# A position-bias network on one Trainium2 core: four keys a group, channels sorted by sign, partial sums added by accumulating transfers

## The chip, the core and the metric

The kernel runs on one core of one Trainium2 chip. TensorE (PE), VectorE (DVE), ScalarE (ACT), GpSimd (POOL) and SyncE (SP) run side by side, each in its own instruction order, and wait for one another by semaphores; transfers run on 16 DMA engines that all queues share. All data are 32-bit floats. The metric is the device time of one launch in microseconds (us), lower is better. A profile is one profiled execution.

## What is computed

The program is a chain of four layers on an image batch of 2 x 512 x 32 x 32. The change is in the first layer, a deformable attention with 2 x 8 heads: 1024 query positions look at 64 sampled keys per head. To the scores a bias is added that a small network computes from the distance of each query to each key:

```python
pos = grid_q[:, :, None, :] - grid_kv[:, None, :, :]         # 16 heads x 1024 x 64 x 2
bias = jnp.sign(pos) * jnp.log1p(jnp.abs(pos))
bias = jax.nn.relu(bias @ cpb_w1 + cpb_b1)                   # 2 -> 128
bias = jax.nn.relu(bias @ cpb_w2 + cpb_b2)                   # 128 -> 128
bias = (bias @ cpb_w3 + cpb_b3)                              # 128 -> 1
sim = jnp.einsum('bhid,bhjd->bhij', qh, kh) + bias
attn = jax.nn.softmax(sim, axis=-1)
```

The 128 -> 128 product, for 16 x 64 x 1024 positions, is the large piece of work here.

## The kernel before

Channels lie on the 128 partitions, the 1024 queries along the free axis. `queries_keys_values` (line 618) comes first: it normalizes x, makes the queries `q_pad` (in the large tile `room`), runs a depthwise convolution on DVE and PE, derives the sampling grid, samples by matmuls (`pkv`), makes the keys `kbd` and the values `val`, and writes the signed logarithms of the distances, which separate into an x part and a y part, to DRAM (`feat`). `first_layer` (line 510) loads these parts back, broadcast to all partitions (tiles `ab`, 64 loads of 512 KB from the SP queue), and scales them by the first layer's weights on ACT.

`biased_scores` (line 827) is the position network. Its loop runs over 8 head pairs p, over j = 0, 2, ... 30, and over 4 turns t (two heads, two halves of 32 keys). One turn treats two keys:

- `hidden` (line 864): for each key DVE adds the x and y parts to a tile of 128 x 1024 (L868); ACT rectifies it (L877), or, for 3 in 16, DVE (L875). Six such tiles are kept.
- `second_layer` (line 880): the 128 output channels are taken in two halves of 64. For a half, the two keys' products lie side by side in one PSUM tile `ph`: four matmuls with 128 x 32 weights fill its four blocks of 32 partitions at the same time (L888; such a group of four is called a set below; each 32-bit matmul of the code stands twice in the trace). There are three `ph` tiles of two banks. ACT rectifies the lower half to `lo` (L898) and the upper half to `hi`, scaled by |w3| (L900); DVE adds lo times the rest of w3 (L901).
- `last_layer` (line 904): a product with a 128 x 32 matrix that is zero but for two columns of signs adds a pair's channels into rows j and j+1 of the PSUM tile `sim` (L909). It is done one step of j late, after turn 1.

At j = 16 the product of queries and keys (`scores`, L921) is added into the same PSUM tile; at the end of a head pair DVE stores it with the bias b3 to `simT` (L931). From the fifth head pair on, softmax steps of the finished ones run beside. The order of PE's instructions is as written in the source; for the other engines a scheduler orders them by an estimate of its own, and each engine then takes its list strictly in order. At j = 16 of the last head pair q is used no more, and `load_weights` loads the next stage's weights (out_w, 1 MB, and mlp_w1, 4 MB) into the same large tile.

Of the kernel before, what the change touches and what calls it, by code (L numbers as in the profile page):

```python
# [72 lines left out]
def constants():  # L73
    p = np.arange(128)
    px, py = (p % 32).astype(np.float32), (p // 32).astype(np.float32)
    neg_y = np.stack([-(py + 4.0 * c) for c in range(8)], axis=1).astype(np.float32)
    j = np.arange(64)
    gx, gy = (j % 8).astype(np.float32), (j // 8).astype(np.float32)

    gj = np.stack([gx, gy]).reshape(2, 1, 4, 16).repeat(16, axis=1)  # L80
    gj = gj.transpose(2, 0, 1, 3).reshape(128, 16)
    line = (2.0 * np.arange(32, dtype=np.float32) / np.float32(31) - 1.0).astype(np.float32)
    groups = np.zeros((128, 128), np.float32)
    for g in range(8):
        groups[16 * g : 16 * g + 16, 16 * g : 16 * g + 16] = 1.0 / 16

    y, x = np.divmod(np.arange(HW), 32)
    taps = np.zeros((HW, 9, 2), np.float32)
    for k in range(9):
        taps[:, k, 0] = y + k // 3 - 1  # L90
        taps[:, k, 1] = x + k % 3 - 1
    taps = taps.reshape(8, 128, 18).transpose(1, 0, 2).reshape(128, 144)
    parts = [
        ("ident", np.eye(128, dtype=np.float32)),
        ("groups", groups),
        ("minus", np.broadcast_to(np.array([0.0, -1.0], np.float32), (128, 2))),
        ("neg_xh", -px[:, None] - np.float32(0.5)),
        ("neg_yh", neg_y - np.float32(0.5)),
        ("gx", np.broadcast_to(gx, (128, 64))),
        ("gy", np.broadcast_to(gy, (128, 64))),  # L100
        ("gj", gj),
        ("line", np.broadcast_to(line, (128, 32))),
    ]
    packed, at = _pack(parts)
    return packed, at, taps


def layouts(i):
# [10 lines left out]
    for name in ("cpb_b2", "cpb_w3"):  # L119

        halves = np.asarray(i["L0_conv_" + name]).reshape(2, 64, 1)
        parts.append((name, np.concatenate([_twice(halves[0]), _twice(halves[1])], axis=1)))
# [20 lines left out]
    cst, cst_at, taps = constants()  # L143
# [8 lines left out]
    for h in range(2):  # L152
# [17 lines left out]
        "w2": np.asarray(i["L0_conv_cpb_w2"]),  # L170
# [106 lines left out]
def layers(net, out):  # L277
# [12 lines left out]
    with ExitStack() as later:  # L290
# [12 lines left out]
        with ExitStack() as l0a:  # L303
# [8 lines left out]
            w2 = keys.tile([128, 128], F32, name="w2_t", tag="w2")  # L312
            first = net.pool(l0a, "cpb_ab", 4)
            parts = queries_keys_values(net, bn, simT, q_flat, q_pad, kbd, val, feat, first)
            nc.sync.dma_start(out=w2, in_=net.ins["w2"])

            def load_weights():
                t = new_room()
                w1 = t[:, : 4 * 2048].rearrange("p (k m) -> p k m", m=2048)
                out_w = t[:, 4 * 2048 :].rearrange("p (k m) -> p k m", m=C)  # L320
                nc.sync.dma_start(out=out_w, in_=net.ins["out_w"])
                nc.sync.dma_start(out=w1, in_=net.ins["mlp_w1"])
                return w1, out_w

            w1, out_w = biased_scores(
                net, q_pad, kbd, feat, w2, simT, first, parts, load_weights
            )
# [290 lines left out]
def queries_keys_values(net, bn, simT, q_flat, q_pad, kbd, val, feat, first):  # L618
# [5 lines left out]
    with ExitStack() as ctx:  # L624
# [15 lines left out]
        with ExitStack() as part:  # L640
# [33 lines left out]

            pd = bank("pd")
# [6 lines left out]
            nc.scalar.activation(g, g, AF.Gelu, bias=net.vec("odw_b"))  # L682

        with ExitStack() as part:
# [61 lines left out]

            for gt, name in grids:
                g3 = gt.rearrange("p (n j) -> p n j", j=64)
                base = net.cst(name).unsqueeze(1).to_broadcast([128, NP, 64])
                nc.vector.scalar_tensor_tensor(g3, g3, 4.0, base, ALU.mult, ALU.add)  # L750
# [55 lines left out]
            for w, out, factor in ((kw, kbd, 64**-0.5), (vw, val, 1.0)):  # L806
                for q in range(2):
# [15 lines left out]
                    )  # L823
    return done


def biased_scores(net, q_pad, kbd, feat, w2, simT, first, parts, load_weights):
# [12 lines left out]
    with ExitStack() as ctx:  # L840
        small = net.pool(ctx, "cpb_w", 1)
        hid1 = net.pool(ctx, "cpb_h1", 6)
        lows = net.pool(ctx, "cpb_lo", 2)
        highs = net.pool(ctx, "cpb_hi", 6)
        ps_h = net.psum(ctx, "cpb_ps_h", 3)
        ps_sim = net.psum(ctx, "cpb_ps_sim", 1)
        w3_lo, w3_hi = net.vec("cpb_w3", 0), net.vec("cpb_w3", 1)
        b2_lo, b2_hi = net.vec("cpb_b2", 0), net.vec("cpb_b2", 1)
        sign = small.tile([128, 1], F32, name="sign", tag="sign")
        nc.vector.tensor_scalar(sign, w3_hi, 0.0, 2.0, ALU.is_ge, ALU.mult)  # L850
        nc.vector.tensor_scalar(sign, sign, 1.0, None, ALU.subtract)
        size = small.tile([128, 1], F32, name="size", tag="size")
        nc.vector.tensor_tensor(size, w3_hi, sign, ALU.mult)
        size_b = small.tile([128, 1], F32, name="size_b", tag="size_b")
        nc.vector.tensor_tensor(size_b, size, b2_hi, ALU.mult)
        low_w = small.tile([128, 1], F32, name="low_w", tag="low_w")
        nc.vector.tensor_tensor(low_w, w3_lo, sign, ALU.mult)

        w3 = small.tile([128, 62], F32, name="w3", tag="w3")
        nc.vector.memset(w3, 0.0)  # L860
        nc.vector.tensor_copy(w3[0:64, 30:31], sign[0:64, :])
        nc.vector.tensor_copy(w3[64:128, 31:32], sign[64:128, :])

        def hidden(i, j, on_vector):
            at_x, at_y = parts[i, j % 32 // 16]
            k = 16 * (j // 32) + j % 16
            h1 = hid1.tile([128, HW], F32, name="h1", tag="h1")
            nc.vector.tensor_tensor(  # L868
                h1.rearrange("p (y x) -> p y x", x=32),
                at_x[:, k : k + 1, :].to_broadcast([128, 32, 32]),  # L870
                at_y[:, k, :].unsqueeze(2).to_broadcast([128, 32, 32]),
                ALU.add,
            )
            if on_vector:
                nc.vector.tensor_scalar(h1, h1, 0.0, None, ALU.max)  # L875
            else:
                nc.scalar.activation(h1, h1, AF.Relu)  # L877
            return h1

        def second_layer(pair):  # L880

            phs = []
            for k in range(2):
                ph = ps_h.tile([128, HW], F32, name="ph", tag="ph")
                for n in range(2):
                    for t in range(4):
                        c0 = 64 * k + 32 * (t % 2)
                        nc.tensor.matmul(  # L888
                            ph[32 * t : 32 * t + 32, half(n)],
                            lhsT=w2[:, c0 : c0 + 32],  # L890
                            rhs=pair[t // 2][:, half(n)],
                            start=True,
                            stop=True,
                            skip_group_check=True,
                        )
                phs.append(ph)
            lo = lows.tile([128, HW], F32, name="lo", tag="lo")
            nc.scalar.activation(lo, phs[0], AF.Relu, bias=b2_lo)  # L898
            hi = highs.tile([128, HW], F32, name="hi", tag="hi")
            nc.scalar.activation(hi, phs[1], AF.Relu, bias=size_b, scale=size)  # L900
            nc.vector.scalar_tensor_tensor(hi, lo, low_w, hi, ALU.mult, ALU.add)  # L901
            return hi

        def last_layer(sim, j, sums):


            for n in range(2):
                for t in range(4):
                    nc.tensor.matmul(  # L909
                        sim[32 * t : 32 * t + 32, half(n)],  # L910
                        lhsT=w3[:, 30 - j : 62 - j],
                        rhs=sums[t][:, half(n)],
                        start=(j == 0),
                        stop=(j == 30),
                        skip_group_check=True,
                    )

        def scores(p, sim):
            for n in range(2):
                for t in range(2):  # L920
                    nc.tensor.matmul(  # L921
                        sim[64 * t : 64 * t + 64, half(n)].rearrange("p (y x) -> p y x", x=32),
                        lhsT=kbd[:, p, 64 * t : 64 * t + 64],
                        rhs=q_pad[:, p, 1 + 16 * n : 17 + 16 * n, 1:33],
                        start=False,
                        stop=False,
# [3 lines left out]
        def store(p, sim):  # L930
            nc.vector.tensor_scalar(simT[:, p, :], sim, net.vec("cpb_b3"), None, ALU.add)  # L931
# [16 lines left out]
        hidden_done = 0  # L948
        for p, j in [(p, j) for p in range(NP) for j in range(0, 32, 2)]:
            if j % 16 == 8:  # L950
                nxt = 2 * p + j // 16 + 1
                if nxt < 2 * NP:
                    parts.update(list(first_layer(net, first, feat, *divmod(nxt, 2)))[-1])
            sums = []
            for t in range(4):
                pair = []
                for k in range(2):
                    key = j + 32 * (t % 2) + k
                    pair.append(hidden(2 * p + t // 2, key, hidden_done % 16 in (3, 8, 13)))
                    hidden_done += 1  # L960
                sums.append(second_layer(pair))
# [6 lines left out]
            elif j == 16:  # L968
                scores(p, sim)
                if p == NP - 1:  # L970
                    weights = load_weights()
            pending = (p, j, sums)
            if p >= CC and j % 8 == 4:
                next(beside, None)
        for _ in beside:
            pass
        last_layer(sim, *pending[1:])
        store(NP - 1, sim)
        return weights
# [1184 lines left out]
```

## Time and profile before

| what | before |
|---|---|
| median of 3 runs (range) | 3835.34 us (3830.59 to 3837.44) |
| span of the profiled execution | 3835.8 us |
| mean granted TensorE clock | 0.992 |
| busy, share of the span: PE, DVE, ACT, POOL | 97%, 72%, 67%, 5% |
| position network, first ph matmul to last sim matmul | 86.6 to 2122.2 us |
| DMA: bytes moved, mean rate | 168.57 MB, 44 GB/s |

The span is the time from the first to the last instruction of the profiled execution. In a row of groups stand the source line, the engine, the operation, the tiles (output <- inputs), the shape and the count; behind the bar the busy time in us, the mean time of one in ns, the idle time of the engine just before such instructions, and what ended most of that. In a row of a timeline stand the start in us, the duration in us, the engine, the line and the count. PEld is the load of weights into TensorE, which overlaps matmuls. In the lines of 40 digits each digit is the busy share, in tenths, of one fortieth of the span.

### The profile page before, as it was taken

The page shows a single profiled execution, that of the slowest core. Times are in us where ns is not written, and L with a number is a line of the kernel's source. Part 1 is how long each engine was busy: PE and PEld are TensorE (multiplying, and loading weights), DVE is VectorE, ACT ScalarE, POOL GpSimd, SP SyncE. Part 2 cuts the span into 40 slices and gives each one's busy share as a digit, 9 for nine tenths or more (in the row PEclk, how much of TensorE's full clock was granted, in tenths as well). Part 3 has the DMA queues.
Part 4 walks back from the last instruction along what each step waited for, and adds up shares of the span by engine and source line. Part 5 has one row for each costly group of instructions (what it writes and reads, how often), then busy time and mean ns, then how long its engine had stood idle before and what let it go on. Part 6 is the DMA issues. An engine that isn't in the chain of part 4 may idle for free. (4 is left out here: it accounts for less than half of the span.)

```text
span 3835.8 us, 59384 instructions
## 1 busy us (share of the span) xinstructions
PE 3739.0 (97%) x25356; PEld 1487.3 (39%) x25356; DVE 2765.5 (72%) x3242; ACT 2566.4 (67%) x2941; POOL 189.1 (5%) x180
## 2 busy tenths in 40 slices
PE   7999999999999999999999999999979999899999
PEld 4532222223222322232323444444434544455555
DVE  6999999999999999999999210411475472566565
ACT  7999999999999999999999221211123243345544
POOL 0000000000000000000000000000261150000000
PEclk9999999999999999999999999999999999999999
DMA  3000000000000000000000100112455481000000
GB/s 111 1 23 23 23 1 23 23 23 12 12 23 23 12 12 23 23 12 12 23 23 34 61 0 0 40 61 77 143 185 173 140 276 42 1 12 1 1 20 25
DMA packets 54459, 168.57 MB, mean 44 GB/s; under 512 B 4804, under 2 KB 10436, under 8 KB 51252
## 3 DMA queue, kind: packets, MB, share of 16 engines
q1 hardware_dynamic: 31556, 83.77, 6.2%
q0 software_dynamic: 21776, 79.14, 6.2%
q8 instruction: 200, 3.28, 0.4%
q10 hardware_dynamic: 864, 1.86, 0.2%
q14 instruction: 63, 0.52, 0.0%
HBM read 156.11 MB, written 8.65 MB: 43 GB/s over the span
## 5 line engine op out<-in xcount | busy, mean ns | idle before, releaser
L888 PE MATMUL ph<-h,w_t 128*32 128x512 f32 x16384 | 1808.0, 593 | 15.7 <-ACT lo L898 6.5
L868 DVE TENSOR_TENSOR h<-ab 128x1024 f32<-128x1024 f32 x1024 | 1206.0, 1219 | 67.2 <-PE ph L888 66.2
L888 PEld LDWEIGHTS ph<-h,w_t 128*32 128x32 f32 x16384 | 547.6, 110 | 1239.9 <-issue 1017.2
L877 ACT ACTIVATE h<-h 128x1024 f32<-128x1024 f32 x832 | 872.1, 1067 | 45.6 <-DVE h L868 42.9
L901 DVE SCALAR_TENSOR_TENSOR hi<-lo,low_w,hi 128x1024 f32<-128x1024 f32 x512 | 654.8, 1279 | 31.6 <-ACT hi L900 30.3
L900 ACT ACTIVATE hi<-ph,size_b,size 128x1024 f32<-128x1024 f32 x512 | 621.3, 1214 | 16.7 <-PE ph L888 12.5
L898 ACT ACTIVATE lo<-ph,vec_t 128x1024 f32<-128x1024 f32 x512 | 571.8, 1117 | 5.8 <-PE ph L888 5.4
L2086 ACT ACTIVATE e<-pl,m 128x1024 f32<-128x1024 f32 x128 | 143.6, 1122 | 228.9 <-DVE m L2078 228.9
L1567 PE MATMUL po<-fold,turned 128*128 128x512 f32 x576 | 266.1, 606 | 3.2 <-DVE dfacc L1575 2.9
L2078 DVE TENSOR_REDUCE m<-pl 128x1 f32<-128x1024 f32 x128 | 150.7, 1219 | 147.2 <-PE pl L1988 147.2
L1135 ACT ACTIVATE h<-ph,vec_t 128x512 f32<-128x512 f32 x64 | 44.0, 687 | 312.0 <-PE ph L1127 311.5
L909 PE MATMUL sim<-hi,w 128*32 128x512 f32 x2048 | 251.0, 592 | 0.0
L1127 PE MATMUL ph<-xn,room 128*128 128x512 f32 x512 | 230.9, 594 | 0.0
L1116 PE MATMUL acc<-h,mlp_w_t 128*128 128x512 f32 x512 | 229.8, 592 | 0.0
L1514 DVE SCALAR_TENSOR_TENSOR sum<-got,wts,sum 128x256 f32<-128x256 f32 x432 | 184.4, 478 | 48.8 <-ACT sum L1510 46.4
L1490 POOL DMA_INDIRECT got<-table,idx x144 | 175.0, 1215 | 554.9 <-DVE sum L1514 268.0
L2040 PE MATMUL pt<-cst_t,e 128*128 128x128 f32 x1024 | 149.3, 279 | 6.6 <-ACT aT L2051 4.0
L2040 PEld LDWEIGHTS pt<-cst_t,e 128*128 128x128 f32 x1024 | 118.6, 142 | 93.6 <-issue 61.3
L1567 PEld LDWEIGHTS po<-fold,turned 128*128 128x128 f32 x576 | 106.6, 195 | 112.4 <-issue 107.4
L1116 PEld LDWEIGHTS acc<-h,mlp_w_t 128*128 128x128 f32 x512 | 97.3, 190 | 122.5 <-issue 122.0
L1127 PEld LDWEIGHTS ph<-xn,room 128*128 128x128 f32 x512 | 96.6, 191 | 117.7 <-issue 117.1
L1541 ACT COPY turned<-pt 128x512 f32<-128x512 f32 x72 | 41.9, 582 | 143.8 <-PE pt L1535 143.6
(250 smaller groups left out, 2711.6 us busy)
## 6 DMA issues: line engine op xcount, KB each, us to landing
ab<-feat_d SPq DMA_DIRECT2D x64, 512.0 KB, 4.0
room<-in_dc_w_dram SPq DMA_DIRECT2D x9, 1024.0 KB, 4.8
dc_w_t<-in_dc_w_dram SPq DMA_DIRECT2D x5, 1024.0 KB, 5.3
room<-in_mlp_w_dram SPq DMA_DIRECT2D x1, 4096.0 KB, 15.6
mlp_w_t<-in_mlp_w_dram SPq DMA_DIRECT2D x1, 4096.0 KB, 12.5
dc_w_t<-in_dc_w_dram SPq DMA_DIRECT2D x8, 512.0 KB, 5.0
w_qkv_t<-in_w_qkv_dram SPq DMA_DIRECT2D x3, 1024.0 KB, 8.6
out_dram<-x_all SPq DMA_DIRECT2D x12, 256.0 KB, 2.0
```

What stands on the lines that cost most here:

```text
L868: nc.vector.tensor_tensor(h1.rearrange("p (y x) -> p y x", x=32), at_x[:, k : k + 1, :].to_broadcast([128, 32, 32]), at_y[:, k, :].unsquee ...
L877: nc.scalar.activation(h1, h1, AF.Relu)
L888: nc.tensor.matmul(ph[32 * t : 32 * t + 32, half(n)], lhsT=w2[:, c0 : c0 + 32], rhs=pair[t // 2][:, half(n)], start=True, stop=True, skip_ ...
L898: nc.scalar.activation(lo, phs[0], AF.Relu, bias=b2_lo)
L900: nc.scalar.activation(hi, phs[1], AF.Relu, bias=size_b, scale=size)
L901: nc.vector.scalar_tensor_tensor(hi, lo, low_w, hi, ALU.mult, ALU.add)
L909: nc.tensor.matmul(sim[32 * t : 32 * t + 32, half(n)], lhsT=w3[:, 30 - j : 62 - j], rhs=sums[t][:, half(n)], start=(j == 0), stop=(j == 30 ...
L1116: nc.tensor.matmul(accs[oc], lhsT=self.w2[:, m, 128 * oc : 128 * oc + 128], rhs=hs[m], start=(m == 0), stop=(m == 15),)
L1127: nc.tensor.matmul(ph, lhsT=self.w1[:, k, 128 * m : 128 * m + 128], rhs=xn[:, k, :], start=(k == 0), stop=(k == CC - 1),)
L1514: nc.vector.scalar_tensor_tensor(t[:, q, :], g[:, s, :], w, t[:, q, :], ALU.mult, ALU.add)
L1567: nc.tensor.matmul(self.out, lhsT=turned[:, at : at + 128], rhs=self.folded.w[k][:, i, :], start=(k == 0 and i == 0), stop=(k == 8 and i = ...
L2040: nc.tensor.transpose(pt[:, 128 * c : 128 * c + 128], e[:, 128 * k : 128 * k + 128], ident)
```

## The change

The network's loop is regrouped, and the second layer's sums are formed in another way.

- **Channels by sign.** A new class `Order` computes on the chip, from w3, a place for each of the 128 channels, so that each quarter of 32 channels can be treated with one rule: quarters 1 to 3 hold, in each of the 32 lanes, channels of one sign of w3, and quarter 0 what is left. |w3| is multiplied into the second layer's weights, which are permuted by a matmul with a 0/1 matrix; the biases and signs are permuted in the same way. This takes some 60 DVE operations on one column, seven small matmuls and two small loads, put among the steps of `queries_keys_values`.
- **Four keys a turn.** j runs in steps of 4. `hidden` makes two keys at once (128 x 2048, six such tiles: three groups deep, five of them in the large tile where q was). `second_layer` makes four PSUM tiles, one for each quarter of channels, with the four keys side by side.
- **Sums.** DVE takes quarter 0 (max with minus the bias, times the sign relation: `lo`), ACT rectifies quarters 1 (`hi`) and 2 (`more`), DVE adds max(quarter 3, minus bias) to `more`. Two transfers issued by GpSimd, which add to their destination, form hi += lo and hi += more; the second is written one group later in the source. What the max form leaves out is a constant, computed once and added at the store.
- **Last layer.** One product for four keys: the 128 x 32 matrix has four columns of signs.
- **Scores.** The products of queries and keys run before the loop, at the end of `queries_keys_values`, are copied to `simT`, and the store adds to them. The large tile is then free for the first layer's tiles.
- **Weights.** out_w is loaded in the last step of the loop, mlp_w1 behind the loop in four parts.

The core of the diff:

```diff
+            for p in range(NP):
+                for n in range(2):
+                    pq = bank("pqk")
+                    for t in range(2):
+                        nc.tensor.matmul(
+                            pq[64 * t : 64 * t + 64, :].rearrange("p (y x) -> p y x", x=32),
+                            lhsT=kbd[:, p, 64 * t : 64 * t + 64],
+                            rhs=q_pad[:, p, 1 + 16 * n : 17 + 16 * n, 1:33],
...
+                    (nc.vector.tensor_copy, nc.scalar.copy)[n](simT[:, p, half(n)], pq)
...
+        def hidden(i, j, at):
+
+            at_x, at_y = parts[i, j % 32 // 16]
+            k = 16 * (j // 32) + j % 16
+            h1 = place(at).rearrange("p (k i) -> p k i", k=2)
+            nc.vector.tensor_tensor(
+                h1.rearrange("p k (y x) -> p k y x", x=32),
+                at_x[:, k : k + 2, :].unsqueeze(2).to_broadcast([128, 2, 32, 32]),
+                at_y[:, k : k + 2, :].unsqueeze(3).to_broadcast([128, 2, 32, 32]),
+                ALU.add,
+            )
+            nc.scalar.activation(h1, h1, AF.Relu)
+            return [h1[:, k, :] for k in range(2)]
+
+        def quarter(quad, q):
+            ph = ps_h.tile([128, HW], F32, name="ph", tag="ph")
+            for n in range(2):
+                for t in range(4):
+                    nc.tensor.matmul(
+                        ph[32 * t : 32 * t + 32, half(n)],
+                        lhsT=order.w2[:, 32 * q : 32 * q + 32],
+                        rhs=quad[t][:, half(n)],
...
+        def rectified(ph, q, pool, name):
+            t = pool.tile([128, HW], F32, name=name, tag=name)
+            nc.scalar.activation(t, ph, AF.Relu, bias=order.bias[:, q : q + 1])
+            return t
+
+        def second_layer(quad, late):
+
+            t0 = lows.tile([128, HW], F32, name="lo", tag="lo")
+            nc.vector.tensor_scalar(
+                t0, quarter(quad, 0), order.first, order.low, ALU.max, ALU.mult
+            )
+            total = rectified(quarter(quad, 1), 1, highs, "hi")
+            nc.gpsimd.dma_start(out=total, in_=t0, accum_op=ALU.add)
+            flush(late)
+            more = rectified(quarter(quad, 2), 2, adds, "more")
+            nc.vector.scalar_tensor_tensor(
+                more, quarter(quad, 3), order.floor, more, ALU.max, ALU.add
+            )
+            late.append((total, more))
+            return total
+
+        def flush(late):
+            for total, more in late:
+                nc.gpsimd.dma_start(out=total, in_=more, accum_op=ALU.add)
+            late.clear()
...
         def store(p, sim):
-            nc.vector.tensor_scalar(simT[:, p, :], sim, net.vec("cpb_b3"), None, ALU.add)
+            nc.vector.scalar_tensor_tensor(
+                simT[:, p, :], sim, order.const, simT[:, p, :], ALU.add, ALU.add
+            )
...
-        for p, j in [(p, j) for p in range(NP) for j in range(0, 32, 2)]:
+        late = []
+        slots = list(range(6))
+        for p, j in [(p, j) for p in range(NP) for j in range(0, 32, 4)]:
...
+            if (p, j) == (NP - 1, 28):
+                slots.remove(4)
+                load_out()
             sums = []
             for t in range(4):
-                pair = []
-                for k in range(2):
+                quad = []
+                for k in range(0, 4, 2):
                     key = j + 32 * (t % 2) + k
-                    pair.append(hidden(2 * p + t // 2, key, hidden_done % 16 in (3, 8, 13)))
-                    hidden_done += 1
-                sums.append(second_layer(pair))
+                    quad += hidden(2 * p + t // 2, key, slots[0])
+                    slots.append(slots.pop(0))
+                sums.append(second_layer(quad, late))
                 if t == 1 and pending is not None:
                     last_layer(sim, *pending[1:])
...
+            biased_scores(net, feat, order, simT, first, parts, t, load_out)
+            for k in range(4):
+                nc.sync.dma_start(out=w1[:, k, :], in_=net.ins["mlp_w1"][:, k, :])
```

The buffers: two `lo` tiles, three `more` tiles, seven `hi` tiles, three `ph` tiles as before.

## Prediction

> **What bounds the kernel now.** I read the page first: its slices say which stretch the change is in and which engines are full there.
>
> ```profile
> PE   7999999999999999999999999999979999899999
> DVE  6999999999999999999999210411475472566565
> ACT  7999999999999999999999221211123243345544
> DMA  3000000000000000000000100112455481000000
> ```
>
> A slice is 95.9 us. From the second to the 22nd all three compute engines are at nine tenths and the DMA engines idle: this is the position network, over half the span. Next its groups, in the page's list (count, total busy, mean ns, idle before):
>
> ```profile
> L888 PE MATMUL ph<-h,w_t 128*32 128x512 f32 x16384 | 1808.0, 593 | 15.7 <-ACT lo L898 6.5
> L868 DVE TENSOR_TENSOR h<-ab 128x1024 f32<-128x1024 f32 x1024 | 1206.0, 1219 | 67.2 <-PE ph L888 66.2
> L877 ACT ACTIVATE h<-h 128x1024 f32<-128x1024 f32 x832 | 872.1, 1067 | 45.6 <-DVE h L868 42.9
> L901 DVE SCALAR_TENSOR_TENSOR hi<-lo,low_w,hi 128x1024 f32<-128x1024 f32 x512 | 654.8, 1279 | 31.6 <-ACT hi L900 30.3
> L900 ACT ACTIVATE hi<-ph,size_b,size 128x1024 f32<-128x1024 f32 x512 | 621.3, 1214 | 16.7 <-PE ph L888 12.5
> L898 ACT ACTIVATE lo<-ph,vec_t 128x1024 f32<-128x1024 f32 x512 | 571.8, 1117 | 5.8 <-PE ph L888 5.4
> L909 PE MATMUL sim<-hi,w 128*32 128x512 f32 x2048 | 251.0, 592 | 0.0
> ```
>
> TensorE waits 15.7 us in front of 16384 matmuls: it sets the stage's time, with the other two just behind. The 593 ns is a latency of overlapping matmuls; the rate is in the timeline (start, duration, count) and the slack in the stretch of stages (PE, PEld, DVE, ACT busy):
>
> ```profile
> 2101.38 7.07 PE L888 MATMUL ph<-h,w_t 128*32 128x512 f32 x64
> 2108.27 1.90 PE L909 MATMUL sim<-hi,w 128*32 128x512 f32 x16
> 2109.99 7.05 PE L888 MATMUL ph<-h,w_t 128*32 128x512 f32 x64
> ...
> 500.00:1000.00 500.00, 496.95 (x4590) 147.41 (x4584) 475.25 (x431) 487.26 (x477) 0.00 (x0) 1.00 0.06 18
> ```
>
> From 2101.38 to 2108.27 64 matmuls pass: 6.89/16 = 0.43 us for a set of four side by side. The stage runs from 86.6 (first ph) to 2122.2 (last sim). A pair of keys costs (32+4)/4 = 9 sets, 3.87 us; 512 pairs 1981 us. The 64 L921 matmuls (8 in 1.72 us) add 13.8, the softmax transposes of four head pairs 9.4. That is 2004 of 2035.6 us: 31 us are stalls.
>
> **The change, part by part.** All sums are against this execution, span 3835.8 us, which the median of the runs (3835.34) equals.
>
> Matmuls. The second layer keeps its 16384. The last layer takes four keys instead of two: 2048 become 1024. Four keys then take (64+4)/4 = 17 sets, 7.31 us, where two pairs took 7.74: 256 x 0.43 = 110 us off the engine that sets the end. The L921 matmuls leave the loop: 13.8 more.
>
> DVE, for four keys. Two additions over 2048: 512 elements take 0.69 us (L782) and 1024 take 1.219, so 2048 about 2.28. The first quarter from PSUM as L931 (1024 from PSUM, 1.28). The fourth quarter, PSUM plus SBUF: L1075 takes 0.75 where an SBUF operation of 512 takes 0.69, so 1.28 to 1.34. In all 7.12 to 7.18 us, against 7.31 of PE. Hidden, by 0.13 us only; where it slips, the ph banks hold PE back, as L898 does now.
>
> ACT. Two rectifications over 2048: 0.61 us at 512, 1.067 at 1024, so 1.97; two quarters at 1.117; 0.27 for the ab tiles (64 x 1.22 over 256). 6.45 of 7.31: hidden, with 0.9 us to spare, where before it had none. The stalls of 31 us I keep: DVE is now as near to PE as ACT was.
>
> Stage start. About 60 operations on one column, some 0.1 us apart where the old ones stand (83.9 to 85.7), stand among the DVE's convolution and grid steps, which are on the path: +5 us (bounds 2 and 9). The 64 score matmuls with their copies now run before the loop: +13.8. The first-layer tiles lie where q was, so the first addition waits for the last score matmul, and the first group needs two tiles: 2 x 2.28 + 1.97 = 6.5 us, where 3.4 passed from the last pk matmul (83.3) to the first ph (86.6). Start 86.6 + 5 + 13.8 + 3.2 = 108.6, so +22.
>
> Stage end. The last group's sum must come back from two transfers: about +3 us. SP's loads: out_w is queued 29 us before its use and took 4.8; w1's four parts and then mlp_w_t move behind the loop. 8 MB took 15.6 + 12.5 us before; their readers start 34 and 41 us after the stage's end (2156.0 and 2162.9). Cost 0; without that cover some 15 us.
>
> The transfers. 512 accumulating transfers of 512 KB, issued by GpSimd: nothing like them runs before. In the built program GpSimd's order is strict: lo of a group, more of the same group, lo of the next. The source puts more one group later; the scheduler has moved it forward. "more" waits for the landing of its group's "lo", and behind it on GpSimd stands the next group's "lo". So the least cycle is: more is issued, its bytes move, the next lo's bytes follow on the same engines, land, and free the next more. It has these rows:
>
> ```profile
> got<-table,idx POOLq DMA_INDIRECT x144, 5.3
> out_dram<-x_all SPq DMA_DIRECT2D x12, 256.0 KB, 2.0
> out_dram<-x_all SPq DMA_DIRECT2D x8, 128.0 KB, 1.7
> ...
> 2008.00:2026.00 18.00, 18.00 (x173) 5.43 (x169) 15.19 (x15) 15.30 (x15) 0.00 (x0) 1.00 0.72 292
> 2700.00:3000.00 300.00, 264.89 (x863) 126.61 (x862) 166.36 (x357) 69.85 (x127) 95.40 (x70) 0.95 0.50 166
> ```
>
> A GpSimd issue took 0.94 us with 0.3 between two (the gathers). 128 KB to 256 KB adds 0.3 us to 1.7, so 1.4 is fixed. Cycle = 0.94 + 0.3 + 1.4 + 2X = 2X + 2.6, X being the time of one transfer on all 16 engines. The last two columns are DMA share and GB/s: plain loads moved 292/0.72 = 405 GB/s while busy, gathers of 4 KB rows 166/0.50 = 332. So a plain copy has X = 1.3 to 1.6. An accumulate must read its destination too. The Trainium skill speaks against the change here: "Collectives: The Full Stack", in the section on the bandwidth ceiling, holds that a reduce takes two reads for one write and gets half the rate of a copy; it measured 32.35 GB/s over two engines. By the rows alone, reading hidden: X = 1.6, cycle 5.8, PE's 7.31 stands. By its figure, an estimate: 16.2 GB/s on 16 engines, X = 2.0, cycle 6.6, PE stands. By its rule on this case's rows: X = 2.6 to 3.2, cycle 7.8 to 9.0, and the transfers set the pace. Which it is no row shows. I take X about 2.3 (between the page's own rate and the lower doubling): cycle 7.2, just under PE. Their latency costs nothing below that: lo and hi of a group are done some 6 us after its start, both transfers land by about 18, and the last layer reads them at 3 x 7.31 = 21.9. The 64 ab loads take 0.4 us a group of the same engines (the 5 to 6% share now).
>
> Sum: start +22, loop -110, scores out of the loop -13.8, end +3: -99 us, 3737.
>
> **Rivals.**
> 1. The transfers become the bound. From X = 2.4 the cycle exceeds 7.31; every 0.1 us more costs 256 x 0.2 = 51 us; from X = 2.55 (7.7) the gain of 99 is gone. With the gather row doubled, X = 3.2: cycle 9.0, 256 x 1.69 = 433 more, 4170. At the middle, X = 2.9: 8.4, 4016. For it: GpSimd's blocking order and the skill's rule. Against: a mean share includes the latency of packets, so true X may be lower. That ends slower.
> 2. Accumulation is slower than two reads explain (X of 5 or more, or a descriptor issue of several us): cycle over 12, beyond 4900. No row speaks for it, none excludes it.
> 3. DVE takes PE's place: its 7.18 with a few stalls is 7.4 to 7.5, some 25 to 50 us less gain: 3762 to 3787.
> 4. The stalls vanish, ACT being relieved: 31 us more gain, 3706.
> 5. The start gives it back: that would take 99 us where I find 22 (bounds 19 to 26); not likely.
>
> **How the numbers follow.** PE stays the bound, or nearly (the forecast with rivals 3 and 4; 3706 to 3800): 0.52. Transfers bind gently, ending within 0.2%: 0.03. Rival 1 slower: 0.37. Rival 2: 0.08. 0.2% (8 us) is about what a measurement can tell from no change. Faster 0.52, same 0.03, slower 0.45. The time is that of the likeliest, 3737; its own range is 3706 to 3800. The range runs from 3706 to 4170, the gather row doubled; above lie rival 2 and the worst of rival 1, below little.
>
> **What would show it.** A group's 64 ph matmuls still 0.43 us a set and PE at 99% in the stage: forecast right. PE idle before sim, released by a DMA of hi<-more, or ph waiting for DVE lo that waits for a DMA; GpSimd's issues spaced over 7.3 us: rival 1; the time from issue to landing of hi<-lo decides (under 5.5 us fits, over 7 does not). First ph near 108.6, DVE h near 2.28 us, DVE near 97%. Wrong would be a first ph after 120, a PE gap at the first w1 matmul, or a DVE lagging through other waits than these.

## The result and the profile after

The changed kernel takes 3957.74 us (median of 4 runs, 3950.05 to 3966.92) where the kernel before took 3832.97 us beside it (3829.34 to 3837.44): 1.0327 times as long, 95% interval 1.0309 to 1.0344. The forecast was 3737 us, 99 us less than before. It came out 125 us slower instead, inside the range given, and as the first rival had it.

The slices of the page, as before (a slice is now 98.8 us):

```profile
PE   7999999999999999999999899999988999899999
DVE  7988888888888888888888311410366474566565
ACT  6777777777777777777777221121112233245544
POOL 0122222212122222222222100000143141000000
DMA  3677777776777677767766600012344572000000
```

In the network's stage (second to 23rd slice) DVE fell from nine to eight tenths and ACT from nine to seven, and the DMA engines rose from nothing to seven. PE's digit hides what matters, since 9 stands for all from 90% up. The stretch from 500 to 1000 us tells more (PE, PEld, DVE, ACT, POOL busy, then clock, DMA share, GB/s), with the queue that moves the adding transfers (packets, MB, share of 16 engines):

```profile
500.00:1000.00 500.00, 470.69 (x4120) 143.41 (x4120) 423.50 (x245) 371.11 (x257) 105.81 (x122) 0.99 0.72 143
```

```profile
q0 software_dynamic: 95504, 347.61, 42.3%
```

PE's busy time fell from 496.95 to 470.69 and the matmuls issued in the same time from 4590 to 4120: now all three compute engines wait. The stage runs from the first ph matmul at 104.4 us to the last sim matmul at 2242.9, or 2138.5/256 = 8.35 us for a group of four keys. The forecast had 7.31 for PE and 7.2 for the transfers.

The groups of the stage (busy, mean ns of one, idle before, and what ended most of that):

```profile
L1041 PE MATMUL ph<-room,w_t 128*32 128x512 f32 x13664 | 1860.3, 596 | 80.2 <-DVE lo L1059 34.0
L1028 DVE TENSOR_TENSOR room<-ab 128x2048 f32<-128x2048 f32 x427 | 971.8, 2286 | 190.1 <-PE ph L1041 189.8
...
L1074 POOL DMA_DIRECT2D hi<-more x256 | 219.5, 857 | 1671.7 <-issue 620.4
L1059 DVE TENSOR_SCALAR lo<-ph,floor,low 128x1024 f32<-128x1024 f32 x256 | 342.7, 1339 | 97.5 <-DMA hi<-lo 68.3
...
L1063 POOL DMA_DIRECT2D hi<-lo x256 | 306.4, 1197 | 74.1 <-ACT hi L1053 68.7
...
L1082 PE MATMUL sim<-hi,w 128*32 128x512 f32 x1024 | 188.7, 608 | 65.3 <-DMA hi<-more 65.2
```

The columns behind the second bar tell it. DVE's lo (L1059) waits 68 us for a transfer: there are two lo tiles, and the one it wants is still being read. PE's sim (L1082) waits 65 us for hi<-more. And GpSimd stands 1671.7 us in front of "more" and only 74.1 in front of "lo": its queue moves on only when a "more" may go. Its timeline shows the cycle (start, duration; in brackets the wait before):

```profile
1013.81 0.86 POOL L1074 DMA_DIRECT2D hi<-more  x1 [7.02 <-DVE room L1028]
1014.35 1.21 POOL L1063 DMA_DIRECT2D hi<-lo  x1
1022.66 0.86 POOL L1074 DMA_DIRECT2D hi<-more  x1 [7.11 <-DMA hi<-lo]
1023.20 1.21 POOL L1063 DMA_DIRECT2D hi<-lo  x1
1030.82 0.86 POOL L1074 DMA_DIRECT2D hi<-more  x1 [6.41 <-DVE room L1028]
1031.36 1.21 POOL L1063 DMA_DIRECT2D hi<-lo  x1
```

"more" of a group and "lo" of the next go out together, back to back; then GpSimd stands some 7 us until that lo has landed, and only then the next "more" may go. From one lo to the next it is 8.85 and 8.16 us here. Where the bracket names a DVE addition, the wait is one for several semaphores, and the releaser named is only the event that was last in the record. The sum that a "more" carries was not what was missing: over all 256 groups it had been ready for 8.8 us (median, 1.0 at least) when its "more" was issued, and the data of a "lo" for 6.5 us. After the issues at 1013.81 and 1014.35 the DMA engines are full from 1015.24 to 1020.44, have a share of 0.08 up to 1021.76 and of 0.00 from 1021.80 to 1024.05. So in over 3 of these 8.85 us next to no bytes move, unless loads from the other queue fill the gap, as they did from 1012.95 to 1015.20 (share 0.94).

### The profile page after: what moved, and what is told of

The parts are those of the page before. It is cut to its first block, busy times and chain, and to the rows that moved or that the text cites. A ratio compares the mean times of both kernels' runs of the same rounds, so it can differ in the third digit from the quotient of the medians.

```text
span 3953.9 us, 57067 instructions
## 1 busy us (share of the span) xinstructions
PE 3730.4 (94%) x24348; PEld 1472.7 (37%) x24348; DVE 2647.7 (67%) x2599; ACT 2184.7 (55%) x2118; POOL 635.1 (16%) x692
## 3 DMA queue, kind: packets, MB, share of 16 engines
q0 software_dynamic: 95504, 347.61, 42.3%
## 5 line engine op out<-in xcount | busy, mean ns | idle before, releaser
L1041 PE MATMUL ph<-room,w_t 128*32 128x512 f32 x13664 | 1860.3, 596 | 80.2 <-DVE lo L1059 34.0
L1028 DVE TENSOR_TENSOR room<-ab 128x2048 f32<-128x2048 f32 x427 | 971.8, 2286 | 190.1 <-PE ph L1041 189.8
L1041 PEld LDWEIGHTS ph<-room,w_t 128*32 128x32 f32 x13664 | 530.1, 110 | 1219.2 <-issue 846.6
L1034 ACT ACTIVATE room<-room 128x2048 f32<-128x2048 f32 x427 | 815.5, 1910 | 251.5 <-DVE room L1028 251.3
L1041 PE MATMUL ph<-h,w_t 128*32 128x512 f32 x2720 | 634.2, 594 | 0.2 <-DVE lo L1059 0.2
L1074 POOL DMA_DIRECT2D hi<-more x256 | 219.5, 857 | 1671.7 <-issue 620.4
L1059 DVE TENSOR_SCALAR lo<-ph,floor,low 128x1024 f32<-128x1024 f32 x256 | 342.7, 1339 | 97.5 <-DMA hi<-lo 68.3
L1066 DVE SCALAR_TENSOR_TENSOR more<-ph,floor,more 128x1024 f32<-128x1024 f32 x256 | 327.3, 1278 | 28.6 <-ACT more L1053 22.6
L1063 POOL DMA_DIRECT2D hi<-lo x256 | 306.4, 1197 | 74.1 <-ACT hi L1053 68.7
L1053 ACT ACTIVATE more<-ph,bias 128x1024 f32<-128x1024 f32 x256 | 284.4, 1111 | 51.3 <-PE ph L1041 51.3
L1082 PE MATMUL sim<-hi,w 128*32 128x512 f32 x1024 | 188.7, 608 | 65.3 <-DMA hi<-more 65.2
L1041 PEld LDWEIGHTS ph<-h,w_t 128*32 128x32 f32 x2720 | 175.5, 110 | 111.7 <-issue 109.4
L1028 DVE TENSOR_TENSOR h<-ab 128x2048 f32<-128x2048 f32 x85 | 193.9, 2281 | 0.0
```

Source lines behind the costliest of these rows:

```text
L1028: nc.vector.tensor_tensor(h1.rearrange("p k (y x) -> p k y x", x=32), at_x[:, k : k + 2, :].unsqueeze(2).to_broadcast([128, 2, 32, 32]), a ...
L1041: nc.tensor.matmul(ph[32 * t : 32 * t + 32, half(n)], lhsT=order.w2[:, 32 * q : 32 * q + 32], rhs=quad[t][:, half(n)], start=True, stop=Tr ...
L1053: nc.scalar.activation(t, ph, AF.Relu, bias=order.bias[:, q : q + 1])
L1059: nc.vector.tensor_scalar(t0, quarter(quad, 0), order.first, order.low, ALU.max, ALU.mult)
L1063: nc.gpsimd.dma_start(out=total, in_=t0, accum_op=ALU.add)
L1066: nc.vector.scalar_tensor_tensor(more, quarter(quad, 3), order.floor, more, ALU.max, ALU.add)
```

## The experiments

The theory (A in the expectations) was that the two chained transfers on GpSimd's strict queue set the pace, as in rival 1. Other causes to be told apart were VectorE's in-order work (rival 3), a slow accumulate (rival 2) and SBUF or DMA contention. How much one transfer takes of all 16 engines, X, is read from the queue's share: the gathers of the later stage alone make 6.3% of 3769.1 us = 237 us, so X = (42.3% of 3953.9 us - 237)/512 = 2.80 us in the changed kernel. In its lists of additions, lo and sums DVE has the same order, operation for operation, in the changed kernel and in the next four; ACT's list too is the same in all five.

**Both transfers left out.**

```diff
-            nc.gpsimd.dma_start(out=total, in_=t0, accum_op=ALU.add)
...
-            for total, more in late:
-                nc.gpsimd.dma_start(out=total, in_=more, accum_op=ALU.add)
```

> Leaves both transfers of a group out, so quarters 0, 2 and 3 of the channels are computed but never added to the bias. Theory A (the chain of transfers, 8.3 us a group, sets the loop's time and nothing else in the change does): TensorE is the bound again at 7.31 us a group, 3720 to 3760 us. Rival B (VectorE, relieved of less than I summed, would bind at about the same pace): still 3850 or more, with VectorE over 97% busy in the loop. Rival C (the longer start and end ate the gain): still over 3800 with TensorE at 99% in the loop.

Measured 3771.02 us (3769.79 to 3771.95), ratio to before 0.9842 [0.9825, 0.9858]. So the transfers cost 3957.7 - 3771.0 = 187 us, and the change without them is faster than before. But 34 us above the forecast remain, without any transfer.

**Plain copies, and half the bytes.** Two kernels: the first without `accum_op`, the second with `[:, :512]` on both sides of both transfers.

> The two transfers copy instead of adding (hi is overwritten, the sum is lost); bytes written, instructions, order and waits stay. Theory A (an adding transfer occupies the engines about twice as long as a copy because it reads its destination as well): a transfer falls from about 2.8 us of all engines to about 1.5, the cycle from 8.3 to about 5.6, TensorE binds, 3720 to 3770 us. Rival D (the cycle is fixed latency of issue and landing on GpSimd): within 1% of 3958.

> The two transfers add only the first 512 of 1024 columns (the other half of the sums is left out). Theory A (time of a transfer goes with its bytes): 1.4 us each, cycle about 5.4 us, TensorE binds, 3720 to 3770 us. Rival D (fixed latency): within 1% of 3958. Rival E (cost by packets, not bytes: 128 rows either way): also near 3958, with a DMA share that stays at 0.7.

Measured 3786.46 us, ratio 0.9884 [0.9867, 0.99], and 3787.67 us, ratio 0.9889 [0.9873, 0.9906]: both above the upper end expected, for the reason that still stood open after the kernel without transfers, and 171 us below the changed kernel. The two queue lines, copies first:

```profile
q0 software_dynamic: 95504, 347.61, 23.8%
```

```profile
q0 software_dynamic: 95504, 213.39, 27.1%
```

Bytes and packets of the copies are those of the changed kernel, and the share is 23.8 instead of 42.3%: X = (23.8% of 3784.7 - 237)/512 = 1.30 us for a copy. By this measure adding takes about 2.2 times as long. Half the bytes take (27.1% of 3783.9 - 237)/512 = 1.54 us, 0.55 of 2.80: the cost goes with the bytes, and there is no large fixed price of an adding transfer, so rival 2 falls. A share could count packets that wait, so the packet records are a second measure: from first to last packet, a transfer that runs alone takes 1.44 us as a copy and 1.53 when it adds half the bytes (medians; 2.77 for a whole adding one, in the kernel below with one transfer a group). By the formula of the prediction the cycles are 5.2 and 5.7 us; both are below PE's pace, and both kernels ran at the same time.

**The same transfers in another order.** The whole computation; "lo" of the next group is put ahead of the older "more".

```diff
-            nc.gpsimd.dma_start(out=total, in_=t0, accum_op=ALU.add)
-            flush(late)
+            added = nc.gpsimd.dma_start(out=total, in_=t0, accum_op=ALU.add)
+            with net.tc.issue_after(added.ins):
+                flush(late)
```

> The whole computation. GpSimd is made to issue the next group's lo transfer before the more transfer of the group before, as the source has it, so that more no longer stands waiting in front of it. Theory A1 (the blocking order on GpSimd sets the cycle of 2X + 2.6; the engines alone need only 2X + 0.4 = 6.0 us a group): TensorE or VectorE bind, 3740 to 3800 us, DMA share of the loop near 0.8. Rival A2 (the engines themselves are full, their share of 0.72 hides idle that cannot be used): 3900 or more, GpSimd still waiting for landings over 5 us a group.

Measured 3811.13 us (3806.83 to 3812.95), ratio 0.9943 [0.9926, 0.9959]: bytes, packets and X (2.78) are unchanged, and 147 us are gone. Its stretch and its GpSimd timeline:

```profile
500.00:1000.00 500.00, 485.92 (x4404) 140.81 (x4404) 451.89 (x262) 398.77 (x276) 113.33 (x130) 1.00 0.77 154
```

```profile
1004.46 0.85 POOL L1063 DMA_DIRECT2D hi<-lo  x1 [5.47 <-ACT hi L1053]
1004.99 1.21 POOL L1075 DMA_DIRECT2D hi<-more  x1
1011.67 0.85 POOL L1063 DMA_DIRECT2D hi<-lo  x1 [5.47 <-ACT hi L1053]
1012.21 1.21 POOL L1075 DMA_DIRECT2D hi<-more  x1
```

GpSimd now waits for data (ACT's hi), no longer for a landing: a "lo" goes out 0.3 us after its data are there (median), where it was 6.5. The group's "lo" has had a whole group's time to land when its "more" comes up. So it was not the bytes, 2 x 2.8 = 5.6 us of 7.55, that exceeded PE's time, but the bytes plus the time in which the queue stood: landing, waking, issue, start. It missed the expected 3740 to 3800 by 11 us. The waits show a further price (total, times, longest):

```profile
PEld ph L1041 <- ACT more L1053: 47.0, 32, 2.9
ACT ab L535 <- DMA ab<-feat_d: 44.1, 21, 5.1
```

The ab loads share the 16 engines. Their median from issue to landing is 4.0 us before, 6.1 in the changed kernel, 8.1 here. The scheduler had placed their scaling on ACT right behind the load, a whole block of 16 groups ahead of its use; ACT, in order, stood up to 5.1 us for it, and PE behind ACT. The changed kernel has this wait as well: 43.4 us in all, where it is 1.2 without the transfers.

**The scaling put late.** On top of that order, each of the four scalings of a block goes into one of the last four groups before its use.

```diff
-                    parts.update(list(first_layer(net, first, feat, *divmod(nxt, 2)))[-1])
+                    coming = next(first_layer(net, first, feat, *divmod(nxt, 2)))
...
+                if j % 16 == 12 and nxt < 2 * NP:
...
+                    with net.tc.issue_after(relus[-1]):
+                        nc.scalar.activation(
+                            tile, tile, AF.Identity, bias=bias, scale=net.vec("cpb_w1", a)
+                        )
```

> The whole computation. On top of the reordered transfers (3811, where ScalarE stood 44 us in front of the scaling of ab tiles whose loads landed after 8.1 us instead of 4.0), each scaling is put into the last four groups of a block of 16, a whole block behind its load, one a group. If those waits are what is left of the transfers' cost above the 3771 without them: ACT's wait for DMA ab falls to near 0, PE's wait for ACT more (68 us) to under 20, and the time to 3772 to 3795. If the full DMA engines (share 0.77) hold the loop back in another way, for instance by SBUF traffic slowing the compute engines, the time stays at 3800 to 3815.

Measured 3789.71 us (3787.32 to 3791.99), ratio 0.988 [0.9863, 0.9896], as expected, and the best version of the whole computation: 46 us faster than before, 168 faster than the changed kernel. ACT's wait for the loads is gone, though they land no sooner (8.2 us). Only 19 us are left to the kernel without transfers, at a DMA share of 0.79: by itself this traffic costs the compute engines no more than that.

**One transfer a group.** `more` is added by a DVE operation instead of the second transfer.

```diff
-            flush(late)
...
-            late.append((total, more))
+            nc.vector.tensor_tensor(total, total, more, ALU.add)
             return total
```

> The whole computation with one transfer a group: lo comes by the transfer, the sum of the third and fourth quarter is added by VectorE. The DMA cycle is then 2.8 + 1.9 = about 4.7 us, far under PE's 7.31, and the DMA share falls from 0.72 to about 0.4. If only the transfers held the loop back and VectorE were free, the time would be about 3740 to 3770. But VectorE takes one operation of 1024 elements more, 1.22 us a group: 7.1 + 1.2 = 8.3 us, above PE, so by my account of the engines 256 x 0.7 us over the 3771 without transfers: 3950 to 3990, about the same as with two transfers, with VectorE busy at 0.98.

Measured 3972.45 us (3970.5 to 3975.53), ratio 1.0361 [1.0343, 1.0378], as expected. X is 2.78 again ((23.9% of 3968.7 - 237)/256) and the DMA share 0.37, but DVE is the bound: 481.51 of 500 us busy, and 49 us of the whole kernel it stands for the landing of the one transfer before it can add. So the second transfer is worth having, as long as it doesn't block the first: with both, the best order took 3790.

**What the 34 us without transfers are.** The last layer comes once in four groups. From one sim to the next the kernels without transfers, with the new GpSimd order and with the late scaling show the same time, their most frequent one: 30.2 us for four groups, where their 68 sets take 68 x 0.43 = 29.2. First I took half of lo's work from DVE, with the transfers left out:

```diff
-                t0, quarter(quad, 0), order.first, order.low, ALU.max, ALU.mult
+                t0[:, half(0)], quarter(quad, 0)[:, half(0)], order.first, order.low, ALU.max, ALU.mult
```

> Leaves out both transfers and half the columns of the first quarter's eviction. Without the transfers the loop took 7.6 us a group where 17 sets of matmuls take 7.31, 34 us above the forecast of 3737. Theory: VectorE, with about 7.1 us of work a group in a strict order, evicts late, and PE waits for it (250 us of PEld waits for DVE more and lo, in pieces of 1.5 us). Then 0.6 us a group less of VectorE work brings the loop to about 7.35 us a group, the time to 3715 to 3745, and PE's wait for DVE lo falls by more than half. Rival: PE's loop takes longer for a reason of its own, as gaps in its weight loads or issue; then the time stays at 3762 to 3772.

Measured 3760.98 us, ratio 0.9812 [0.9795, 0.9828]: only 10 us better, and the 30.2 still there (sim at 1023.92, the next at 1054.16), so the amount of DVE's work as such is not what holds PE. But its timeline shows the place:

```profile
1002.49 2.29 DVE L1028 TENSOR_TENSOR room<-ab 128x2048 f32<-128x2048 f32 x1 [2.18 <-PE ph L1041]
...
1004.70 1.28 DVE L1065 SCALAR_TENSOR_TENSOR more<-ph,floor,more 128x1024 f32<-128x1024 f32 x1
...
1006.03 0.11 PEld L1041 LDWEIGHTS ph<-room,w_t 128*32 128x32 f32 x2 [1.05 <-DVE more L1065]
```

DVE has been idle for 2.18 us when PE finishes a group. What it does then is an addition for a later group, which wanted the tile that the group set free; the sum of this group's fourth quarter, ready at the same moment, is queued behind it. Addition 2.29 and sum 1.28 end after 3.5 us, and PE, which has two other ph tiles (2 x 8 sets = 3.44 us), stands about 0.32 us: its sets start 0.75 us apart here (1005.28 and 1006.03) instead of 0.43. The 1.05 in the bracket is the gap between weight loads. Three such stalls in four groups make 30.2 out of 29.2.

**The sum queued ahead of that addition,** with and without the transfers (`mores` holds the sums, one a group):

```diff
-            nc.vector.tensor_tensor(
+            with net.tc.issue_after(mores[-3]) if len(mores) > 2 else ExitStack():
+                nc.vector.tensor_tensor(
```

> The whole computation. In the reordered kernels the loop runs at exactly 30.2 us for four groups (7.55 a group) whether the transfers are there or not, where 68 sets of matmuls take 29.2: three times in four groups TensorE stands 0.32 us in front of a bank that VectorE's sum of the fourth quarter (more) frees late. VectorE has that sum queued behind an addition of a later group, 2.28 us long, which waits for the same last matmuls to free its tile. Here, on top of the reordered transfers and loads (3790), an addition stands behind the sum of the group whose tile it takes. If the order is the cause: four groups in 29.2 to 29.5 us, PE's wait for DVE more under 40 us (178 before), and the time to 3727 to 3750. If VectorE's amount of work is the cause, or the DMA traffic: 3780 to 3795.

> Leaves both transfers out, and has the same order on VectorE: the addition stands behind the sum of the group whose tile it takes. Without the transfers and in the old order it took 3771. If the order on VectorE makes the 34 us between that and the forecast of 3737, it is 3710 to 3740 here; if not, 3765 to 3775. Its distance to the whole computation in the same order is what the transfers cost beside a full PE: 10 to 25 us by the theory that only their place in the queues matters, near 0 or negative by none.

Measured 3810.46 us, ratio 0.9934 [0.992, 0.9947], and 3803.74 us, ratio 0.9918 [0.9903, 0.9933]: both miss the range for the theory by 60 us and more, lie above that for its rival too, and are 21 and 33 us worse than in the old order. The edit did not do what it was meant to: the addition it holds back goes behind the sum, but in 203 and 214 of 256 groups another addition now stands directly before the sum, where it was 254. In DVE's list the order changed to addition, lo, addition, sum, and the waits of the kernel without transfers show a new one:

```profile
DVE more L1068 <- ACT more L1056: 169.7, 127, 2.9
PEld ph L1044 <- ACT hi L1056: 145.2, 179, 2.7
PEld ph L1044 <- DVE lo L1062: 119.8, 108, 2.1
```

DVE now stands in order for ACT, and PE for hi and lo. ACT in turn stands 47.4 us for the ab loads in this kernel, though no transfer slows them: where the scheduler puts the scaling is enough for that. The attempt neither proves nor refutes the chain, since it shortened the stalls (29.9 for four groups, where it went best) and put larger ones elsewhere.

**The same order in the changed kernel.** The edit just shown, and nothing else:

> The whole computation, the changed kernel with nothing but the new order on VectorE; both transfers stand in GpSimd's queue as in the changed kernel, each of more waiting for its lo and the next lo behind it. If that cycle of two transfers, 8.35 us a group, sets the pace, VectorE's order is worth nothing here: 3945 to 3965 where the changed kernel took 3958. If VectorE held it back, 3890 to 3920.

Measured 3939.5 us, ratio 1.0271 [1.0256, 1.0287]: 18 us better than the changed kernel, 5 us below the range expected and far from the 3890 to 3920 that DVE's holding it back would give. The DMA share is again 0.72, and GpSimd's waits in front of "more" are again most of its time. The order on DVE is a small term there.

**The same work taken away at the other place.** Transfers left out, and of one addition in two only 24 of 32 rows. DVE has 0.51 us less to do in a group (249 of 512 additions take 1758 instead of 2281 ns), nearly as much as with the halved lo, 0.53 (804 instead of 1339 ns). The shortened addition is the one directly before the sum, in 240 of 256 groups.

```diff
-                h1.rearrange("p k (y x) -> p k y x", x=32),
+                h1.rearrange("p k (y x) -> p k y x", x=32)[:, :, :rows, :],
```

> Leaves out both transfers and a quarter of one first-layer addition in two (24 rows of 32): VectorE does 0.54 us a group less, as much as in the kernel with the halved lo (3761), but at the place that TensorE waits for: this addition takes the tile that the last matmuls of a group set free, and the sum of the same group's fourth quarter is queued behind it. If that chain (last matmul, addition of 2.28 us, sum of 1.28, bank free 0.32 us late) holds TensorE, shortening it by 0.53 removes the stall: four groups fall from 30.2 to 29.2 to 29.5 us, the time to 3725 to 3745. If the floor of 30.2 has another cause, or is the mere amount of VectorE work, it stays at 3758 to 3768 as with the halved lo.

Measured 3700.76 us (3699.17 to 3706.09), ratio 0.9656 [0.9641, 0.9671]: 70 us less than without the transfers alone, 60 less than with the halved lo. Stretch, two sim rows, and PE's wait for the sum, with the halved lo and here:

```profile
500.00:1000.00 500.00, 500.00 (x4664) 150.58 (x4660) 441.11 (x277) 420.47 (x290) 0.00 (x0) 1.00 0.06 18
```

```profile
1027.16 1.90 PE L1083 MATMUL sim<-hi,w 128*32 128x512 f32 x16
...
1056.34 1.90 PE L1083 MATMUL sim<-hi,w 128*32 128x512 f32 x16
```

```profile
PEld ph L1041 <- DVE more L1065: 177.6, 171, 1.6
PEld ph L1045 <- DVE more L1069: 91.6, 173, 1.1
```

29.18 us for four groups, PE busy 500.00 of 500, and each wait for the sum shorter by about 0.5 us, which the halved lo did not change (179.7 without transfers alone). DVE's order differs from that of the kernel without transfers in 16 of 1024 places, with the halved lo in as many. The same saving on DVE is worth 10 us off the chain and 70 on it. So PE's stalls come from the chain last matmul, addition, sum, ph tile, not from the amount of DVE's work. What was not shown is a whole computation in which a new order alone removes them.

**Seven tiles instead of six,** in the best version:

```diff
-        adds = net.pool(ctx, "cpb_add", 3)
-        highs = net.pool(ctx, "cpb_hi", 7)
-        sixth = net.pool(ctx, "cpb_h1")
+        adds = net.pool(ctx, "cpb_add", 2)
+        highs = net.pool(ctx, "cpb_hi", 6)
+        sixth = net.pool(ctx, "cpb_h1", 2)
...
-        slots = list(range(6))
+        slots = list(range(7))
```

> The whole computation: the reordered transfers and loads (3790) with seven first-layer tiles of 2048 instead of six (one buffer less each for more and for the sums, to make room). An addition then takes a tile that was free some 3.7 us earlier, so it need not start at the end of a group's matmuls, and the sum queued behind it is not late. If that dependence sets the floor of 30.2 us for four groups, it falls to 29.2 to 29.6 and the time to 3735 to 3765; if only the strict order on VectorE matters, which stays the same, or if the scarcer buffers bring waits of their own, 3780 to 3810.

Measured 3801.07 us (3798.95 to 3807.36), ratio 0.9917 [0.9903, 0.993], 11 us worse. DVE's order stayed addition, sum, and the addition again waits for PE's last matmuls; apparently the scheduler used the seventh tile to run one addition further ahead. The time for four groups stayed 30.2, and ACT's more waited 125 us for the scarcer buffers (DMA hi<-more). A version of the whole computation at 29.2 was not found.

## Why the prediction was wrong

The step that failed is "I take X about 2.3 ... cycle 7.2, just under PE": the term X, the time of one adding transfer, was taken too small. It measured 2.80, and with it the transfers, not PE, set the pace of the loop. The form of the sum held: with 2.80 its 2X + 2.6 gives 8.2 us, and the loop took 8.35 a group. The whole sum then gives 3737 + 256 x (8.2 - 7.31) = 3965, where 3958 was measured. Point by point:

- **The cycle's form.** GpSimd's strict order, "more" behind the landing of its "lo", the next "lo" behind that: right. Undoing only this order took away 147 of the 187 us that the transfers cost.
- **The size of X.** Three candidates were set side by side: the rows alone 1.6; 2.0, an estimate from the figure of the Trainium skill ("Collectives: The Full Stack", section "The bandwidth ceiling"); and its rule (a reduce reads twice for one write, so gets half the rate) on this case's rows, 2.6 to 3.2. The measurement is 2.80 against 1.30 for the copy (2.77 and 1.44 from first to last packet): the ratio of about two held, the figure carried over did not (512 KB/16/2.80 us = 11.7 GB/s per engine, where it gave 16.2). That it is the second read that costs, no run here shows. I took a value between the figure and the lower doubling, which no candidate gave. The cycle crosses PE's time at X = 2.4; the doubling of this case's own rows lay wholly above. That was rival 1, given 0.37, and it is what came.
- **"A mean share includes the latency of packets, so true X may be lower".** This argument against rival 1 held for the copy, whose 1.30 lies at the lower end of 1.3 to 1.6, but it could not carry the forecast: this lower end doubled is 2.6, still above 2.4.
- **Matmuls: "17 sets, 7.31 us".** Right as a bound, reached only with the shortened addition (29.18 us for four groups). PE's work fell as said; in the whole computation its waits outweighed that, or in the best order ate about half of the forecast gain (46 us are left of 99).
- **DVE 7.12 to 7.18, "hidden, by 0.13 us only; where it slips, the ph banks hold PE back".** The work was 2 x 2.286 + 1.339 + 1.278 = 7.19, and it slipped. Without transfers the kept 31 us of stalls became 75 (stage 103.6 to 2058.6 us, less 1871 for matmuls and 9.4 for transposes), 44 more; with the addition shortened they are 5 (106.8 to 1992.5). Rival 3 named 25 to 50 us for this and had the wait right; the reason is the place of one operation in the order, not the amount of work.
- **ACT 6.45.** The busy rows give about 6.3; it had the time to spare. (The 0.27 for the ab tiles was a slip: 64 x 1.22/256 is 0.31.) That it would stand in order for the ab loads, slowed by the transfers, I had not seen: their 0.4 us a group was counted as a load on the engines, not as a later landing with ACT behind it. Taking it away was worth 21 us in the kernel with the new order.
- **Start and end.** First ph at 104.4, not 108.6 (+18 instead of +22). From the start of the last sim matmul to the end it is 1711.0 us after and 1714.2 before: the moved weight loads cost nothing, as said.
- **The named check.** For issue to landing of hi<-lo the page gives no figure. The packet records give 6.5 us from issue to last byte (median), and the page of the kernel with only DVE's order changed, where GpSimd has the same order, gives 6.8. That lies between the 5.5 that would fit and the 7 that would not, so this sign alone did not decide. The others did: PE idle before sim, released by hi<-more, and ph waiting for a lo that waits for a transfer.

The gap of 221 us between 3957.7 and 3737 is thus: 147 the order of the transfers on GpSimd, 21 ACT standing for loads that the transfers delay, 19 the rest of the transfers' cost, not taken apart (part of it is the wait for the last sums at the stage's end, part a start 3 us later), and 34 what the kernel without transfers still took above the forecast. The first three are differences between runs in this sequence; with the mends in another order their shares could differ. The 34 are a net sum: 44 us more of stalls, on the DVE chain as far as is shown, less some 10 us for a shorter start and end.

## What to carry to other kernels

A transfer that adds is not a copy: here it took about twice the copy's time. Where it has not been measured, work with that doubling too, and when a bound is crossed between the candidates, don't take the middle for the forecast. Two dependent transfers on a strict queue cost their bytes plus the landing between them; putting another group's transfer into that gap took away 147 of 187 us here, with the same bytes. When an engine is near its bound, look at what is queued in front of the operation that frees a buffer: half a microsecond there was worth 70 us, the same half elsewhere 10.

## What was not expected of the hardware

- An adding transfer of 512 KB inside SBUF took 2.80 us of all 16 DMA engines, a copy of the same bytes and packets 1.30.
- GpSimd's issue of it took 0.857 us, with half the bytes 0.856, and of a plain copy 0.528: adding costs issue time too.
- At a DMA share of 0.77 and 0.79 the loads from the other queue landed after 8.1 and 8.2 us (median) instead of 4.0, though the engines were not full; with seven tiles, at 0.79 too, it was 6.6, so the share alone does not set it.
